# Turning the softmax's shares with VectorE and DMAs instead of TensorE in a one-core transformer block

## The chip, the cores and the metric

The kernel runs on one core of a Trainium2 chip. The metric is the device time of one execution in microseconds, the median of three runs. All data are float32. Engine names in the profile's lines: PE is TensorE (PEld its weight loads), DVE is VectorE, ACT is ScalarE, POOL is GpSimd, SP is SyncE, which here only issues DMAs (SPq in the timeline).

## The reference

A block of four layers on x of 8 x 512 x 256. The change touches the first, an attention with 16 query heads of 64 and one shared key and value head, a learned bias by relative position, a causal limit, and one "null" key and value ahead of the sequence:

```python
# per sequence b: x normalized over its 256 columns, then
q = l2norm(xn @ Wq) * q_scale          # (16, 512, 64)
k = l2norm(xn @ Wkv[:, :64]) * k_scale # (512, 64), one head for all
v = xn @ Wkv[:, 64:]                   # (512, 64)
# a null key and value (from cond_64) stand ahead of the sequence
sim  = 8 * q @ concat(null_k, k).T + concat(null_bias, rel_pos_bias)
attn = softmax(where(mask & causal, sim, -big))   # (16, 512, 513)
out  = layernorm((attn @ concat(null_v, v)) @ Wout) * g_out
```


## The kernel before, in words

Attention comes first and takes the time up to about 950 us; the delta rule and the experts share the rest. Attention works on tiles of 128 queries: 8 sequences, 4 tiles each (t = 0 to 3). Because of the causal limit a tile has n = (t + 1) * 128 keys. A tile's 8 pairs of heads are cut into steps of max(1, 4 // (t + 1)) pairs: 2, 4, 8 and 8 steps for the four tiles, 22 a sequence, 176 in all. A step handles some 1024 columns a partition (768 for t = 2): 2 * pairs heads, n keys each.

`attention_plan` writes the order out by hand. `units` holds the steps under way. `step(k)` calls, in this order: `attention_weights_turned` for step k, the due work of k - 0.5, `attention_softmax` for step k + AHEAD - 1, `attention_values` for step k - 1, `attention_scores` for step k + AHEAD, and the due work of k. Due work (queries, keys, normalizing, division, projection) is put at fractions of steps with `at(...)`. VectorE, ScalarE, SP and TensorE keep this order (class `Ordered`, and `a.mm` and `a.turn`, whose instructions all carry lines L125, L131 and L132); GpSimd's order is the scheduler's.

The steps' parts and their tiles:

- `attention_scores`: GpSimd adds bias and mask row into a_bm (L450, 3 buffers). TensorE multiplies turned queries a_qT by turned keys a_kT into two PSUM tiles a_s. VectorE adds a_bm and takes the minimum over each row in one instruction per head (the sign is turned round), into a_pr and a_mn.
- `attention_softmax`: ScalarE takes the exponential in place in a_pr, one instruction per head, with the row sums in a_rs.
- `attention_weights_turned`: TensorE turns every 128 x 128 block of a_pr (keys on partitions afterwards) into the PSUM tile a_ptp, two banks; ScalarE copies one half to a_pT, VectorE the other.
- `attention_values`: TensorE multiplies the values in a_kv by a_pT into a_av (PSUM), keys as the contracted dimension.
- `attention_shares`, `attention_shares_spread`, `attention_divided`: for each half of a tile's heads the inverse row sums are turned on TensorE into a_rp, copied to a_rT, written to DRAM (a_rd) by SP, and read back broadcast over 64 partitions, twice (a_rep, two issues on SP). VectorE multiplies a_av by a_rep into a_oT. `w.half` and `w.last` are the steps that end the halves.

A DMA that SP issues waits for the DMA eight issues before it on SP's queue (eight semaphores in turn). SP's queue also carries the loads of x and of the mask for the next sequence, and the stores of the layer's result hT.

Of the kernel before, what the change touches and what calls it, by code (L numbers as in the profile page):

```python
# [10 lines left out]
F32 = mybir.dt.float32  # L11
U8 = mybir.dt.uint8
AF = mybir.ActivationFunctionType
ALU = mybir.AluOpType
AX = mybir.AxisListType
PSUM = bass.MemoryType.PSUM
DRAM = bass.MemoryType.DRAM

P = 128
B, S, D = 8, 512, 256  # L20
NT = S // P
# [113 lines left out]

AHEAD = 3
KVW = 2 * DH + H1


def attention_setup(g, ctx, asides):
# [8 lines left out]
    a.wk = ctx.enter_context(tc.tile_pool(name="a_wk", bufs=2))  # L151
    a.sm = ctx.enter_context(tc.tile_pool(name="a_sm", bufs=3))
    a.s = ctx.enter_context(tc.tile_pool(name="a_s", bufs=4, space=PSUM))
    a.bias = wp.tile([P, H1, S], F32, name="a_bias")
    a.ks = wp.tile([P, 1], F32, name="a_ks")
    a.vw = wp.tile([H1, D], F32, name="a_vw")
    by_k = "(c p) n -> p c n"
# [1 line left out]
    with tc.tile_pool(name="as_c", bufs=1) as sp, tc.tile_pool(name="as_w", bufs=2) as wk, tc.tile_pool(  # L159
# [13 lines left out]
        w2 = sp.tile([P, NCT, H1], F32, name="as_w2")  # L173
        nc.scalar.dma_start(out=w2, in_=ins["c_w2"].rearrange(by_k, p=P))
        attention_plan(g, a, asides)
        a.run(-27)
        a.wkv = wp.tile([P, NCT, KVW], F32, name="a_wkv")
        a.sync.dma_start(out=a.wkv[:, :, 0 : 2 * DH], in_=ins["c_Wkv"].rearrange(by_k, p=P))
        a.wq = wp.tile([P, NCT, H1 * DH], F32, name="a_wq")
# [82 lines left out]
            )  # L262
            nc.vector.tensor_reduce(a.wkv[:, c, 2 * DH : KVW], wn, AX.X, ALU.add)

        a.run(-4)


        for h in range(H1):
            hk = wk.tile([P, S], F32, tag="hk", name="as_hk", bufs=4)
            row = gd[h]  # L270
            eng = a.sync if h % 2 else nc.scalar
            eng.dma_start(out=hk, in_=bass.AP(tensor=row.tensor, offset=row.offset, ap=[[1, P], [1, S]]))
            bp = ps.tile([P, 512], F32, tag="tp", name="as_bp")
            nc.tensor.matmul(bp, g.flip, hk, start=True, stop=True)
            nc.scalar.copy(a.bias[:, h, :], bp)


        nvb = sp.tile([P, 8 * H1], F32, name="as_nvb")
# [8 lines left out]
        nc.vector.tensor_copy(a.vw, vps[0:H1, 0:D])  # L287

    a.pp = ctx.enter_context(tc.tile_pool(name="a_pp", bufs=4))
    a.tr = ctx.enter_context(tc.tile_pool(name="a_tr", bufs=2, space=PSUM))  # L290
    a.av = ctx.enter_context(tc.tile_pool(name="a_av", bufs=2, space=PSUM))
    return a


def stats(g, a, x, mv, t):
# [39 lines left out]
def attention_norm(g, a, s):  # L335

    nc, b = a.nc, s.b
    r, mr = center(g, a, s.mv, "a_n")
    for t in range(NT):
        nc.scalar.activation(s.x[:, t, :], s.x[:, t, :], AF.Identity, bias=mr[:, t : t + 1], scale=r[:, t : t + 1])  # L340
    s.mrow = a.xp.tile([P, S], F32, tag="mrow", name=f"a_mrow{b}")
    nc.gpsimd.tensor_scalar(s.mrow, s.mk, 1.0, -BIG, ALU.subtract, ALU.mult)


def attention_turned(g, a, s):
# [33 lines left out]
def attention_keys_turned(g, a, s):  # L379
    nc = a.nc  # L380
    tp = a.s.tile([P, S], F32, tag="s", name="a_ktp")
    for t in range(NT):
        a.turn(tp[:, t * P : (t + 1) * P], s.kn[:, t].rearrange("p i d -> p (i d)"), g.ident)
    s.kT = a.xp.tile([P, S], F32, tag="kT", name=f"a_kT{s.b}")
    nc.scalar.activation(s.kT, tp, AF.Copy, scale=a.ks)
    s.hn = a.xp.tile([P, NT, D], F32, tag="hn", name=f"a_hn{s.b}")


# [36 lines left out]
def attention_queries_turned(g, a, w, half):  # L425

    nc = a.nc
    if half == 0:
        w.qT = a.wk.tile([P, 8, P], F32, tag="qT", name="a_qT")
        w.rs = a.sm.tile([P, H1], F32, tag="rs", name="a_rs")  # L430
        w.mn = a.sm.tile([P, H1], F32, tag="mn", name="a_mn")
        w.pn = a.sm.tile([P, H1], F32, tag="pn", name="a_pn")
        w.avs, w.rep = [None, None], [None, None]
    qf = w.q.rearrange("p h d -> p (h d)")
    tp = a.s.tile([P, 4, P], F32, tag="s", name="a_qtp")
    for i in range(4):
        cc = half * 4 + i
        a.turn(tp[:, i, :], qf[:, cc * P : (cc + 1) * P], g.ident)
    nc.scalar.copy(w.qT[:, half * 4 : half * 4 + 4, :], tp)


def attention_scores(g, a, w, c0, pairs):

    nc, s, t = a.nc, w.s, w.t
    n = (t + 1) * P
    u = SimpleNamespace(w=w, c0=c0, pairs=pairs, n=n)

    bm = a.pp.tile([P, 2 * S], F32, tag="bm", name="a_bm", bufs=3)
    bm = bm[:, 0 : 2 * pairs * n].rearrange("p (h m) -> p h m", m=n)
    nc.gpsimd.tensor_tensor(  # L450
        bm,
        a.bias[:, 2 * c0 : 2 * (c0 + pairs), (NT - 1 - t) * P :],
        s.mrow[:, 0:n].unsqueeze(1).to_broadcast([P, 2 * pairs, n]),
        ALU.add,
    )
    sps = [a.s.tile([P, S], F32, tag="s", name="a_s") for _ in range(2)]
    for j in range(pairs):
        for i in range(2):
            pi = slice(i * DH, (i + 1) * DH)
            a.mm(sps[i][:, j * n : (j + 1) * n], w.qT[pi, c0 + j, :], s.kT[pi, 0:n], start=True, stop=True)  # L460
    pr = a.pp.tile([P, 2 * S], F32, tag="pr", name="a_pr", bufs=5)
    u.pr = pr[:, 0 : 2 * pairs * n].rearrange("p (h m) -> p h m", m=n)
    for j in range(2 * pairs):
        h = 2 * c0 + j
        nc.vector.tensor_tensor_reduce(
            out=u.pr[:, j, :],
            in0=sps[j % 2][:, j // 2 * n : (j // 2 + 1) * n],
            in1=bm[:, j, :],
            scale=1.0,
            scalar=w.sn[:, h : h + 1],  # L470
            op0=ALU.add,
            op1=ALU.min,
            accum_out=w.mn[:, h : h + 1],
        )
    return u


def attention_softmax(g, a, u):
    nc, w = a.nc, u.w
    for j in range(2 * u.pairs):  # L480
        h = 2 * u.c0 + j
        nc.scalar.activation(
            u.pr[:, j, :], u.pr[:, j, :], AF.Exp, bias=w.mn[:, h : h + 1], scale=-1.0, accum_out=w.rs[:, h : h + 1]
        )


def attention_weights_turned(g, a, u):

    nc, n, kt, w = a.nc, u.n, u.n // P, u.w

    u.room = max(2, u.pairs)
    first = u.c0 % u.room
    if first == 0:
        w.pT = a.pp.tile([P, 4 * S], F32, tag="pT", name="a_pT", bufs=2)[:, 0 : 2 * u.room * n].rearrange(
            "p (i j m) -> p i j m", i=2, m=n
        )
    u.pT = w.pT
    m = u.pairs * n
    for i in range(2):
        tp = a.tr.tile([P, S], F32, tag="tr", name="a_ptp")  # L500
        for j in range(u.pairs):
            for k in range(kt):
                o = (j * kt + k) * P
                a.turn(tp[:, o : o + P], u.pr[:, 2 * j + i, k * P : (k + 1) * P], g.ident)
        copy = nc.vector.tensor_copy if i else nc.scalar.copy
        copy(u.pT[:, i, first : first + u.pairs], tp[:, 0:m].rearrange("p (j m) -> p j m", m=n))
    u.whole = first + u.pairs == u.room


def attention_values(g, a, u):  # L510

    w, kt = u.w, u.n // P
    c0 = u.c0 + u.pairs - u.room
    if c0 % 4 == 0:
        w.avs[c0 // 4] = a.av.tile([P, 4, P], F32, tag="av", name="a_av")
    for k in range(kt):
        for i in range(2):
            a.mm(
                w.avs[c0 // 4][i * DH : (i + 1) * DH, c0 % 4 : c0 % 4 + u.room, :],
                w.s.kv[:, k, DH : 2 * DH],  # L520
                u.pT[:, i, :, k * P : (k + 1) * P],
                start=k == 0,
                stop=k == kt - 1,
            )


def attention_shares(g, a, w, half):
# [10 lines left out]
def attention_shares_spread(g, a, w, half):  # L538
# [4 lines left out]
    rT = a.sm.tile([8, P], F32, tag="rT", name="a_rT")  # L543
    nc.scalar.copy(rT, tp[0:8, 0:P])
    rd = g.dram.tile([8, P], F32, tag="a_rd", name="a_rd", bufs=4)
    nc.sync.dma_start(out=rd, in_=rT)
    w.rep[half] = a.wk.tile([P, 4, P], F32, tag="rep", name="a_rep")
    for i in range(2):
        nc.sync.dma_start(out=w.rep[half][i * DH : (i + 1) * DH], in_=rd[i::2].partition_broadcast(DH))


def attention_divided(g, a, w, half):
# [42 lines left out]
def attention_plan(g, a, asides):  # L595
# [17 lines left out]
    def at(k, f, *args):  # L613
        due.setdefault(k, []).append((f, args))

    for w in tiles:
        b, t, s = w.s.b, w.t, w.s
        at(w.half - 2, attention_shares, w, 0)
        at(w.half - 0.5, attention_shares_spread, w, 0)
        at(w.half + 1, attention_divided, w, 0)  # L620
        at(w.last - 2, attention_shares, w, 1)
        at(w.last - 0.5, attention_shares_spread, w, 1)
        at(w.last + 1, attention_divided, w, 1)
        at(w.last + 1, attention_null_turned, w)
        at(w.last + 3, attention_projected, w)
        for half in range(2):
            at(w.first - 9 + half, attention_queries, w, half)
            at(w.first - 7.5 + half, attention_queries_normed, w, half)
            at(w.first - 5 + half, attention_queries_turned, w, half)
        if t == 0:  # L630
            at(w.first - 27, attention_load, s)
            for i in range(NT):
                at(w.first - 25 + i, attention_stats, s, i)
            at(w.first - 21, attention_norm, s)
            at(w.first - 16, attention_turned, s)
            at(w.first - 14, attention_keys, s)
            at(w.first - 10, attention_keys_turned, s)
        at(w.last + 5, attention_out_stats, s, t)
        if t == NT - 1:
            at(w.last + 5, attention_out_norm, s)  # L640
# [12 lines left out]
                a.outs.append(out)  # L653

    def step(k):
        if 0 <= k < len(steps):
            attention_weights_turned(g, a, units[k])
        given(k - 0.5)
        if 0 <= k + AHEAD - 1 < len(steps):
            attention_softmax(g, a, units[k + AHEAD - 1])  # L660
# [1437 lines left out]
```

## Time and profile before

| | us |
|---|---|
| Median of three runs (lowest to highest) | 2442.67 (2441.17 to 2445.53) |
| The profiled execution | 2440.13 |
| Its span | 2438.0 |
| Busy in the span: PE / DVE / ACT / POOL | 2294.3 / 1428.8 / 986.5 / 1126.6 |
| Span's mean granted TensorE clock | 0.969 |

The span is the time from the first to the last instruction of the profiled execution. Durations in lines of groups are ns for one instruction; "busy" is the union of a group's instructions. Matmuls are pipelined, so a group's busy time is less than its count times its mean. "Idle before" is the time its engine stood still just ahead of the group's instructions, with what ended that. A timeline line has its start, the duration, the engine, the line of the kernel and what is written from what. DMA issues are not counted as busy.

### The profile page before, as it was taken

The page shows a single profiled execution, that of the slowest core. Times are in us where ns is not written, and L with a number is a line of the kernel's source. Part 1 is how long each engine was busy: PE and PEld are TensorE (multiplying, and loading weights), DVE is VectorE, ACT ScalarE, POOL GpSimd, SP SyncE. Part 2 cuts the span into 40 slices and gives each one's busy share as a digit, 9 for nine tenths or more (in the row PEclk, how much of TensorE's full clock was granted, in tenths as well). Part 3 has the DMA queues.
Part 4 walks back from the last instruction along what each step waited for, and adds up shares of the span by engine and source line. Part 5 has one row for each costly group of instructions (what it writes and reads, how often), then busy time and mean ns, then how long its engine had stood idle before and what let it go on. Part 6 is the DMA issues. An engine that isn't in the chain of part 4 may idle for free.

```text
span 2438.0 us, 53093 instructions
## 1 busy us (share of the span) xinstructions
PE 2294.3 (94%) x20726; PEld 1686.7 (69%) x20726; DVE 1428.8 (59%) x4016; ACT 986.5 (40%) x2706; POOL 1126.6 (46%) x1420
## 2 busy tenths in 40 slices
PE   4899999999999997769899999999999999999999
PEld 2456665565666554547777788888887877888887
DVE  4456667665766675656646557467466466443433
ACT  2667666665766653333233323323223322311111
POOL 3677768677777762343324325225225234232211
PEclk8999999999999998769999999999999999999999
DMA  3201012010111014112323423334334134232433
GB/s 101 61 14 46 24 36 61 27 33 32 37 33 36 19 31 96 55 31 62 69 71 86 105 71 107 84 81 110 77 88 124 48 92 119 61 118 81 118 98 96
DMA packets 347082, 166.97 MB, mean 68 GB/s; under 512 B 195328, under 2 KB 325120, under 8 KB 346832
## 3 DMA queue, kind: packets, MB, share of 16 engines
q1 hardware_dynamic: 343824, 160.16, 24.4%
q10 hardware_dynamic: 3008, 3.43, 0.5%
q8 instruction: 163, 2.67, 0.5%
q14 instruction: 87, 0.71, 0.1%
HBM read 148.33 MB, written 15.18 MB: 67 GB/s over the span
## 4 chain that ended last, share of the span: by engine, by line
PE 72%; DVE 13%; DMA 5%; POOL 5%; ACT 2%; issue 2%; SPq 0%; ACTq 0%; DVEq 0%; POOLq 0%
PE m_guf L131 12%; PE m_gue L131 8%; PE m_accf L131 6%; PE a_op L131 6%; PE a_s L131 5%; PE a_av L131 5%; PE a_ptp L132 4%; PE a_qp L131 4%; PE m_acce L131 4%; PE d_pp L131 4%; DVE d_y L125 2%; PE d_op L131 2%; POOL a_bm L450 1%; DMA d_Uh<-d_hU 1%; PE d_cop L131 1%
## 5 line engine op out<-in xcount | busy, mean ns | idle before, releaser
L450 POOL TENSOR_TENSOR a_bm<-a_bias,a_mrow 128x1024 f32<-128x1024 f32 (+1 forms) x176 | 381.9, 2171 | 85.7 <-DVE a_mn L125 73.2
L131 PE MATMUL m_guf<-m_oute,m_wf 128*128 128x256 f32 x1536 | 370.9, 385 | 4.5 <-DVE m_hf L125 2.4
L131 PEld LDWEIGHTS m_guf<-m_oute,m_wf 128*128 128x128 f32 x1536 | 285.8, 191 | 58.5 <-issue 10.1
L131 PE MATMUL m_gue<-m_xT,m_we 128*128 128x256 f32 x1280 | 311.6, 387 | 3.2 <-DVE m_he L125 2.8
L125 DVE CUSTOM_DVE_ANT_0 a_pr<-a_s,a_bm,a_sn 128x512 f32<-128x512 f32 (+3 forms) x512 | 254.2, 545 | 68.9 <-PE a_s L131 53.5
L125 ACT ACTIVATE a_pr<-a_pr,a_mn 128x512 f32<-128x512 f32 (+3 forms) x512 | 282.0, 554 | 17.5 <-DVE a_mn L125 16.9
L125 POOL TENSOR_TENSOR m_hf<-m_hf,m_ctf 128x256 f32<-128x256 f32 x128 | 97.0, 759 | 374.5 <-DVE m_hf L125 186.2
L131 PEld LDWEIGHTS m_gue<-m_xT,m_we 128*128 128x128 f32 x1280 | 236.7, 191 | 39.5 <-DVE m_he L125 5.8
L125 DVE SCALAR_TENSOR_TENSOR m_tf<-m_tf,m_guf 128x256 f32<-128x256 f32 x192 | 80.4, 419 | 289.7 <-ACT m_tf L125 289.3
L125 POOL TENSOR_TENSOR m_he<-m_he,m_cte 128x256 f32<-128x256 f32 x128 | 104.6, 817 | 232.2 <-DVE m_he L125 106.7
L125 ACT ACTIVATE m_tf<-m_guf 128x256 f32<-128x256 f32 x192 | 73.4, 383 | 338.0 <-PE m_guf L131 333.4
L131 PE MATMUL a_s<-a_kT,a_qT 64*128 64x384 f32 (+3 forms) x1024 | 200.0, 471 | 6.3 <-DVE a_mn L125 6.0
L131 PE MATMUL m_accf<-m_hf,m_wf 128*128 128x256 f32 x768 | 197.4, 380 | 2.0 <-DVE m_outf L125 1.1
L132 PE MATMUL a_ptp<-table,a_pr 128*128 128x128 f32 x1280 | 179.7, 278 | 20.4 <-DVE a_pT L125 19.4
L132 PEld LDWEIGHTS a_ptp<-table,a_pr 128*128 128x128 f32 x1280 | 145.7, 142 | 75.2 <-issue 29.5
L125 DVE TENSOR_TENSOR m_te<-m_gue,m_te 128x256 f32<-128x256 f32 x160 | 67.6, 423 | 221.6 <-ACT m_te L125 221.6
L125 ACT ACTIVATE m_te<-m_gue 128x256 f32<-128x256 f32 x160 | 61.2, 382 | 294.7 <-PE m_gue L131 294.7
L131 PE MATMUL a_av<-a_pT,a_kv 128*64 128x256 f32 (+1 forms) x1216 | 167.0, 406 | 2.9 <-DVE a_pT L125 2.8
L131 PE MATMUL m_acce<-m_he,m_we 128*128 128x256 f32 x640 | 163.7, 381 | 0.6 <-issue 0.6
L131 PEld LDWEIGHTS m_accf<-m_hf,m_wf 128*128 128x128 f32 x768 | 145.7, 190 | 22.7 <-POOL m_hf L125 1.8
L131 PEld LDWEIGHTS a_s<-a_kT,a_qT 64*128 64x128 f32 x1024 | 84.0, 187 | 81.7 <-issue 40.2
L131 PEld LDWEIGHTS m_acce<-m_he,m_we 128*128 128x128 f32 x640 | 121.4, 191 | 18.0 <-issue 1.0
(343 smaller groups left out, 4076.8 us busy)
## 6 DMA issues: line engine op xcount, KB each, us to landing
a_rep<-a_rd SPq DMA_DIRECT2D x128, 128.0 KB
m_cte<-m_combe SPq DMA_DIRECT2D x64, 256.0 KB
m_ctf<-m_combf SPq DMA_DIRECT2D x128, 128.0 KB
m_we<-in_e_w_gate_dram SPq DMA_DIRECT2D x64, 128.0 KB
m_we<-in_e_w_up_dram SPq DMA_DIRECT2D x64, 128.0 KB
m_we<-in_e_w_down_dram SPq DMA_DIRECT2D x64, 128.0 KB
m_wf<-in_f_gate_w_dram SPq DMA_DIRECT2D x128, 64.0 KB
m_wf<-in_f_up_w_dram SPq DMA_DIRECT2D x128, 64.0 KB
```

Source lines behind the costliest of these rows:

```text
L125: return lambda *args, **kw: tc.keep_in_program_order(f(*args, **kw))
L131: mm = lambda *args, **kw: tc.keep_in_program_order(pe.matmul(*args, **kw))
L132: turn = lambda *args: tc.keep_in_program_order(pe.transpose(*args))
L450: nc.gpsimd.tensor_tensor(bm, a.bias[:, 2 * c0 : 2 * (c0 + pairs), (NT - 1 - t) * P :], s.mrow[:, 0:n].unsqueeze(1).to_broadcast([P, 2 * p ...
```

## The change

The blocks of a_pr are no longer turned on TensorE. VectorE turns each 32 x 32 block in place in a_pr (one instruction a step), and DMAs within SBUF bring the blocks to the other quarters of 32 partitions: quarter q and block b of a_pr go to partitions of quarter b in a_pT, 16 DMAs of 32 partitions for every two steps. So that whole blocks lie together, the keys are taken in another order: key k of every 128 lies in block k // 32, and bias, mask row, turned keys, a_bm and a_pr have a dimension of four blocks. a_pr covers two steps (3 buffers of 4 * S columns, before 5 of 2 * S), a_bm has 2 buffers, a_pT still 2. The turning runs for step k + AHEAD - 2 with AHEAD = 4, at the head of step k; the two PSUM banks of a_ptp go to a_av. The write of a_rd moves to ScalarE's queue, the two a_rep issues become a function of their own one step later (`attention_shares_brought`), and due work ahead of the steps moves up by one.

```diff
-AHEAD = 3
+AHEAD = 4
...
-            nc.scalar.copy(a.bias[:, h, :], bp)
+            nc.scalar.copy(quarters(a.bias[:, h]), by_block(bp))
...
-    a.tr = ctx.enter_context(tc.tile_pool(name="a_tr", bufs=2, space=PSUM))
-    a.av = ctx.enter_context(tc.tile_pool(name="a_av", bufs=2, space=PSUM))
+    a.av = ctx.enter_context(tc.tile_pool(name="a_av", bufs=4, space=PSUM))
...
+def by_block(x):
+    return x.rearrange("p (k b e) -> p b k e", b=4, e=CK)
+def quarters(x):
+    return x.rearrange("p b (k e) -> p b k e", e=CK)
...
 def attention_scores(g, a, w, c0, pairs):
...
-    u = SimpleNamespace(w=w, c0=c0, pairs=pairs, n=n)
-
-    bm = a.pp.tile([P, 2 * S], F32, tag="bm", name="a_bm", bufs=3)
+    u = SimpleNamespace(w=w, c0=c0, pairs=pairs, n=n, room=2 * pairs)
+    u.first = c0 % u.room
+    u.whole = u.first + pairs == u.room
+
+    bm = a.pp.tile([P, 2 * S], F32, tag="bm", name="a_bm", bufs=2)
...
-    pr = a.pp.tile([P, 2 * S], F32, tag="pr", name="a_pr", bufs=5)
-    u.pr = pr[:, 0 : 2 * pairs * n].rearrange("p (h m) -> p h m", m=n)
+    if u.first == 0:
+        pr = a.pp.tile([P, 4 * S], F32, tag="pr", name="a_pr", bufs=3)
+        w.pr = pr[:, 0 : 2 * u.room * n].rearrange("p (b h e) -> p b h e", b=4, h=2 * u.room)
+    u.pr = w.pr
...
 def attention_weights_turned(g, a, u):
-    for i in range(2):
-        tp = a.tr.tile([P, S], F32, tag="tr", name="a_ptp")
-        for j in range(u.pairs):
-            for k in range(kt):
-                o = (j * kt + k) * P
-                a.turn(tp[:, o : o + P], u.pr[:, 2 * j + i, k * P : (k + 1) * P], g.ident)
-        copy = nc.vector.tensor_copy if i else nc.scalar.copy
-        copy(u.pT[:, i, first : first + u.pairs], tp[:, 0:m].rearrange("p (j m) -> p j m", m=n))
...
+    nc, w = a.nc, u.w
+    x = u.pr[:, :, 2 * u.first : 2 * (u.first + u.pairs), :].rearrange("p b h e -> p b (h e)")
+    nc.vector.transpose(x, x)
+    if u.whole:
+        u.pT = a.pp.tile([P, 4 * S], F32, tag="pT", name="a_pT", bufs=2)[:, 0 : 2 * u.room * u.n].rearrange(
+            "p (q h e) -> p q h e", q=4, h=2 * u.room
         )
+        for q in range(4):
+            for b in range(4):
+                nc.sync.dma_start(
+                    out=u.pT[b * CK : (b + 1) * CK, q].rearrange("p h e -> p (h e)"),
+                    in_=u.pr[q * CK : (q + 1) * CK, b].rearrange("p h e -> p (h e)"),
+                )
...
-    nc.sync.dma_start(out=rd, in_=rT)
+    nc.scalar.dma_start(out=rd, in_=rT)
+    w.rd[half] = rd
+
+
+def attention_shares_brought(g, a, w, half):
     w.rep[half] = a.wk.tile([P, 4, P], F32, tag="rep", name="a_rep")
     for i in range(2):
-        nc.sync.dma_start(out=w.rep[half][i * DH : (i + 1) * DH], in_=rd[i::2].partition_broadcast(DH))
+        a.nc.sync.dma_start(out=w.rep[half][i * DH : (i + 1) * DH], in_=w.rd[half][i::2].partition_broadcast(DH))
...
-        at(w.half - 2, attention_shares, w, 0)
-        at(w.half - 0.5, attention_shares_spread, w, 0)
-        at(w.half + 1, attention_divided, w, 0)
+        at(w.half - 3, attention_shares, w, 0)
+        at(w.half - 1.5, attention_shares_spread, w, 0)
+        at(w.half - 0.5, attention_shares_brought, w, 0)
+        at(w.half + (1 if t else 2), attention_divided, w, 0)
...
     def step(k):
-        if 0 <= k < len(steps):
-            attention_weights_turned(g, a, units[k])
+        if 0 <= k + AHEAD - 2 < len(steps):
+            attention_weights_turned(g, a, units[k + AHEAD - 2])
```

The second half's due times (`w.last`) move in the same way, except that its division stays at `w.last + 1`. `attention_values` works on the larger a_pT: up to four pairs of heads a matmul, read in runs of 32.

## The prediction

> **What bounds the kernel now.** I read the page first (busy shares, slices), then the windows of the attention stage, then its groups, and last the DMA issues of SP's queue, since the change moves work there. The stage runs from about 85 to 950 us:
>
> ```profile
> core 0: us, PE busy (x) PEld busy (x) DVE busy (x) ACT busy (x) POOL busy (x), PEclk, DMA share, GB/s
> 85.00:950.00 865.00, 830.15 (x5065) 510.83 (x5065) 577.16 (x1696) 551.36 (x1661) 617.66 (x660) 0.99 0.12 34
> ```
>
> PE is busy for 830 of 865 us at a granted clock of 0.99; POOL (618), VectorE (577) and ScalarE (551) have room. There are 22 steps a sequence, 8 sequences, so 176 steps. I count in pairs of steps, because the changed kernel moves its data once for two: 88 pairs, 865/88 = 9.83 us each. The groups that go are these (after the count: busy us, mean ns, idle before):
>
> ```profile
> L132 PE MATMUL a_ptp<-table,a_pr 128*128 128x128 f32 x1280 | 179.7, 278 | 20.4 <-DVE a_pT L125 19.4
> ```
>
> and the copies of its result on VectorE, by form (ScalarE has as many):
>
> ```profile
> L125 DVE COPY a_pT<-a_ptp 128x512 f32<-128x512 f32 x112 | 75.2, 671 | 25.2 <-PE a_ptp L132 25.1
> L125 DVE COPY a_pT<-a_ptp 128x384 f32<-128x384 f32 x64 | 34.5, 539 | 1.2 <-PE a_ptp L132 1.2
> ```
>
> So the premise holds: the turning costs the bounding engine 180 us. The question is what takes its place. SP's queue in the timeline, beside VectorE's division that needs its result:
>
> ```profile
> 114.97 0.27 SPq L125 DMA_DIRECT2D a_rd<-a_rT  x1
> 116.23 1.24 SPq L125 DMA_DIRECT2D a_rep<-a_rd  x2
> ...
> 119.91 0.69 DVE L125 TENSOR_TENSOR a_oT<-a_av,a_rep 128x512 f32<-128x512 f32 x1 [0.38 <-DMA a_rep<-a_rd]
> ```
>
> The second column is how long SP is held by the issue itself: 0.62 us for one a_rep. VectorE waited for the landing, 119.91 - 117.47 = 2.44 us after the second issue ended. SP does only three such issues in 13 us today. How long SP is held by other shapes (min/median/max ns, from the tiles' views):
>
> ```profile
> L1534 SPq DMA_DIRECT2D m_ctf<-m_combf x128: 444/546/1685, 1248.4 to 2411.9; - x128
> L1534 SPq DMA_DIRECT2D m_cte<-m_combe x64: 319/376/1203, 1118.4 to 2338.6; - x64
> L1651 SPq DMA_DIRECT2D m_combf<-m_cT x8: 330/373/1401, 1245.8 to 2385.4; - x8
> L1651 SPq DMA_DIRECT2D m_combe<-m_cT x8: 292/298/299, 1116.9 to 2306.2; - x8
> ```
>
> All four move rows of 2 KB; they differ in rows: 64, 128, 16 and 8. It is not the bytes that hold SP.
>
> **What goes.** On PE 179.7 us of turning and most of the 20 us before it: 830 - 180 = 650, or 7.4 us a pair. On ScalarE 176 copies (94.7 us), on VectorE 176 (109.7 us). PSUM's two banks for the turning go to a_av.
>
> **What VectorE gets.** One transpose a step, 112 of 128x1024 and 64 of 128x768, in place in SBUF. The trace has no such operation. Nearest rows: the 128x1024 multiply of d_kn at 1.22 us; above it a_q's 128x512 multiply, mean 1.10 us, so 2.2 us for 1024, both from SBUF and lengthened in some places (0.81 to 1.63 us in the timeline); the dearest is one 128x1024 multiply at 3.36 us. Nothing goes below 1.1 us (two PSUM copies of 512 are 1.34). I take 1.22 and 0.95: one input, dense rows. Sum 112 x 1.22 + 64 x 0.95 = 198 us. VectorE then has 577 - 110 + 198 = 665 us, 7.6 us a pair, just over PE's 7.4; POOL stands at 618/88 = 7.0. With the idle that PE has today (4%) a pair bounded by the engines takes 7.9 us, and the stage 695: 170 us gained, if nothing else binds. A rule speaks against the change here: the Trainium skill ("VectorE: DVE Perf Modes", section The three transpose paths) gives 311 ns for a 128x128 turn in blocks of 32, which as my estimate would be 2.5 us for 1024 columns, nearer to the a_q row than to mine. The sum does not use it.
>
> **What SP gets.** After both steps of a pair are turned, 16 DMAs from quarter to quarter, 32 rows of 2 KB (1.5 KB for the third tile): 88 x 16 = 1408 issues, one queue, in order. a_rd (64 issues) moves to ScalarE's queue, about 64 x 0.33 = 21 us on an engine that loses 95, so nothing. The cost of an issue of 32 rows lies between the rows of 16 and of 64 (373 and 546 ns), plus 0.05 us between two issues in a chain: 0.42 to 0.60 us. I take the middle, 0.51; below it stands the 8-row DMA (0.30 + 0.05), above it the chained 64-row ones with a wait, 0.59 + 0.05 = 0.64; each new one carries a wait too, on a DMA eight before it. So 16 issues hold SP 16 x 0.51 = 8.2 us, against 7.9 us for a pair by the engines. The data are the smaller part: 1 MB a pair is 128 GB/s, and the 101 GB/s of the first slice took a DMA share of 0.35.
>
> Another rule speaks for it: the Trainium skill ("DMA: Bandwidth & Descriptors", section Issuing engines are not separate DMA queues) calls the sequencer's time to start a DMA usually small beside the DMA, and the same page's section Anatomy of one DMA has about 50 ns of dispatch, on another issue path. By that figure 16 issues would be 0.8 us (estimate), the engines would bound, and the kernel would take 2270 us. The rows above say 0.3 to 0.6 us, and decide.
>
> **What waits behind SP.** In the built order of the changed kernel SP has, in 56 of the 88 pairs (seven a sequence: two halves in each of four tiles, two of which fall together), 16 a_pT issues, then the two a_rep, then the next pair's a_pT. VectorE's order has the transpose that completes pair m, and before the one that completes pair m+1 stands the division a_oT, which waits for just that a_rep. That closes a loop across two engines: transpose -> 16 issues -> 2 a_rep issues (1.25) -> landing (2.44) -> a_oT (0.69) -> transpose (1.22). So such a pair can't take less than 16p + 5.6 us, where p is the time of one issue; at p = 0.51 it is 13.8 us, and today's whole pair is 9.83. The other 32 pairs take the larger of 7.9 and 16p = 8.2. Loads of x and mask and the stores of hT stand in the same queue, 24 issues in all, inside the error of p. Sum: 56 x 13.8 + 32 x 8.2 = 1035 us in place of 865, +170.
>
> **Edits at nothing.** a_bm is read in four blocks (rows of 128 and of 512 in one block took the same 2.37 us, so I expect no change) and has two buffers instead of three: POOL is then held by VectorE a step earlier; it has 2 to 3 us of room in a pair by the sum above, and if that cover is gone it costs some of the 73 us that it waits for a_mn already, as much again at most. a_av reads runs of 32; fewer and wider matmuls for the second tile, the same columns. VectorE's min-add writes four blocks instead of a row: same elements. The first one of a pair now waits for the DMAs of three pairs before; those are done unless SP is two pairs late. One step more of fill, about 5 us either way. PE will be busy for some 650 of 1035 us; the trace shows what such gaps do: between 975 and 1036 us PE was busy for 44 of 61 us at a granted clock of 0.71. 650/0.71 = 915 us still fits under 1035, so I charge nothing.
>
> **Rivals.**
> 1. SP's loop, p between 0.42 and 0.64 (my forecast). At 0.42: 56 x 12.3 + 32 x 7.9 = 942, +77, so 2517. At 0.64: 56 x 15.8 + 32 x 10.2 = 1211, +346, so 2786. For it: order of the queues and the issue rows. Against: no 32-row issue is in the trace, and none from SBUF to SBUF within it.
> 2. Faster: SP is held so shortly that the loop fits. Break-even is 56(16p + 5.6) + 32 x 7.9 = 865, p = 0.33 us, about what the 8-row DMA shows (0.30 + 0.05). At 0.25 it is 791, -74, 2366; from p = 0.14 down the engines bound, 695, -170, 2270. For it: rows of 8 and 16 are cheap, and the 128-row m_cte (376) is cheaper than the 64-row one, so the cost isn't plain in rows.
> 3. VectorE's transpose at the a_q rate, 2.2 us: the loop becomes 14.8, VectorE 9.6 a pair; 56 x 14.8 + 32 x 9.6 = 1136, +271, 2711.
> 4. Nothing to measure: p falls on the break-even point.
>
> That the change doesn't do what it says is excluded by the built order: no a_ptp is left on PE.
>
> **Numbers.** Chances: first 0.62, third 0.14, second 0.21, fourth 0.03. The profiled execution took 2440.1 us (span 2438.0) and the median of the runs is 2442.7, 2.5 above, so 2440.1 + 170 + 2.5 = 2613. The forecast's own range is 2520 to 2790. The range for 8 in 10 reaches into the second case, down to 2390 (p about 0.28), and up to 2790, which takes in the third. Measurement can tell about 0.2% (5 us) from no change: faster 0.21, same 0.03, slower 0.76.
>
> **What would show it.** Right: SPq a_pT issues of 0.4 to 0.6 us in unbroken rows of 16; VectorE idle before a_oT for a_rep of several us, some 56 times; PE in the stage at 60 to 70%, with a lower clock; transposes near 1.2 us. Wrong: a_oT waits for nothing, or issues under 0.33 us; then the stage ends before 950 us. If PE stays over 90% busy, rival 2 was right.

## The result, and the profile after

The changed kernel takes 2878.97 us (median of four runs, 2876.13 to 2882.34), the kernel before beside it 2443.0 (2441.17 to 2445.53): a ratio of 1.1785, 95% interval 1.177 to 1.1799. It is slower, as predicted, but by 436 us in place of 170, and outside the range. The profiled execution took 2876.5 us, its span 2874.7.

The attention stage, 85 to 952 us before, now ends near 1395 us; what follows it is within 6 us as long as before. The row of the windows for it (the columns are those of the first fence of the prediction):

```profile
85.00:1395.00 1310.00, 853.17 (x3662) 439.05 (x3661) 655.74 (x1702) 480.64 (x1489) 622.58 (x660) 0.79 0.34 87
```

No engine is busy for more than about 65% of the stage. PE's granted clock fell to 0.79, and still PE idles for 457 us. The page's slices show the same as a picture, the first 19 or so being attention:

```profile
PE   5666667566666666666578899999999999999998
PEclk8788888777887788777677999999999999999999
```

What new instructions cost, from the page's groups (us busy, mean ns, idle before) and, for SP, from the tiles' views (min/median/max ns of an issue):

```profile
L462 POOL TENSOR_TENSOR a_bm<-a_bias,a_mrow 128x1024 f32<-128x1024 f32 (+1 forms) x176 | 383.4, 2179 | 167.3 <-DVE a_mn L125 154.9
...
L125 DVE TENSOR_TENSOR a_oT<-a_av,a_rep 128x512 f32<-128x512 f32 x64 | 44.2, 691 | 416.3 <-DMA a_rep<-a_rd 409.4
...
L125 DVE STREAM_TRANSPOSE a_pr<-a_pr 128x1024 f32<-128x1024 f32 (+1 forms) x176 | 198.3, 1127 | 2.8 <-ACT a_pr L125 2.8
```

```profile
L125 SPq DMA_DIRECT2D a_pT<-a_pr x1408: 507/589/1632, 101.7 to 1388.0; - x176
L125 SPq DMA_DIRECT2D a_rep<-a_rd x128: 614/620/661, 111.9 to 1389.3; - x128
```

The transposes are cheap. An a_pT issue is not: 0.589 us, and with the 0.044 between two issues 0.633; a set of 16, the issues of one pair of steps, takes 10.1 us at the median, 10.36 on average. It isn't the wait for the DMA eight issues before that lengthens them: the last of a set has landed 1.4 us (median) after its issue, and the issue eight places later comes 5 us later. The waits name the loop from both ends, VectorE held by a_rep in the group of a_oT above, SP by VectorE here (us, times, longest; the longest, in the later views of this wait too, is that for the first transpose, ahead of the first set):

```profile
SPq L125 <- DVE a_pr L125: 259.2, 55, 19.4
```

One turn of it in the timeline (VectorE's and SP's rows; the bracket is the idle time before):

```profile
763.16 1.19 DVE L125 STREAM_TRANSPOSE a_pr<-a_pr 128x1024 f32<-128x1024 f32 x1
764.49 10.06 SPq L125 DMA_DIRECT2D a_pT<-a_pr  x16
...
774.59 1.29 SPq L125 DMA_DIRECT2D a_rep<-a_rd  x2
...
778.56 0.69 DVE L125 TENSOR_TENSOR a_oT<-a_av,a_rep 128x512 f32<-128x512 f32 x1 [7.96 <-DMA a_rep<-a_rd]
779.28 1.19 DVE L125 STREAM_TRANSPOSE a_pr<-a_pr 128x1024 f32<-128x1024 f32 x1
780.63 10.90 SPq L125 DMA_DIRECT2D a_pT<-a_pr  x16
```

From set to set 16.14 us: 10.1 of issues, 1.3 for a_rep, 2.7 until it has landed, 0.7 division, 1.2 transpose. VectorE stood still for 7.96 us with the next transpose behind the division. SP's rows from 102 to 1390 us fill the stage: sets 911 us, a_rep 83, pauses ahead of sets 250 (55 of them, 4.55 us each), loads, stores and small gaps 44, together 1288. Ahead of these lie 17 us until the first set, behind them 5 us.

### The profile page after: what moved, and what is told of

Read it like the earlier page. It is cut to its first block, busy times and chain, and to the rows that moved or that the text cites. A ratio compares the mean times of both kernels' runs of the same rounds, so it can differ in the third digit from the quotient of the medians.

```text
span 2874.7 us, 52513 instructions
## 1 busy us (share of the span) xinstructions
PE 2311.1 (80%) x19318; PEld 1613.1 (56%) x19318; DVE 1506.0 (52%) x4016; ACT 914.4 (32%) x2530; POOL 1130.3 (39%) x1420
## 4 chain that ended last, share of the span: by engine, by line
PE 40%; SPq 12%; DVE 9%; DMA 5%; issue 2%; ACT 1%; POOL 1%; DVEq 0%; POOLq 0%; ACTq 0%
SPq L125 12%; PE m_guf L131 10%; PE m_gue L131 7%; PE m_accf L131 5%; PE m_acce L131 3%; PE d_pp L131 3%; DMA a_rep<-a_rd 2%; DVE d_y L125 2%; PE d_op L131 1%; DMA d_Uh<-d_hU 1%; PE d_cop L131 1%; PE d_uwp L131 1%; PE d_mp L131 1%; DVE d_subst L125 1%; PE d_pw L131 1%
## 5 line engine op out<-in xcount | busy, mean ns | idle before, releaser
L462 POOL TENSOR_TENSOR a_bm<-a_bias,a_mrow 128x1024 f32<-128x1024 f32 (+1 forms) x176 | 383.4, 2179 | 167.3 <-DVE a_mn L125 154.9
L131 PE MATMUL a_av<-a_pT,a_kv 128*64 128x256 f32 (+1 forms) x1088 | 258.5, 637 | 101.5 <-DMA a_pT<-a_pr 96.4
L132 PE MATMUL a_rp<-table,a_rs 128*8 128x128 f32 x64 | 22.7, 354 | 315.6 <-DVE a_rs L125 309.9
L125 DVE TENSOR_TENSOR a_oT<-a_av,a_rep 128x512 f32<-128x512 f32 x64 | 44.2, 691 | 416.3 <-DMA a_rep<-a_rd 409.4
L131 PE MATMUL a_s<-a_kT,a_qT 64*128 64x384 f32 (+3 forms) x1024 | 237.8, 535 | 6.4 <-DVE a_mn L125 4.7
L131 PEld LDWEIGHTS a_av<-a_pT,a_kv 128*64 128x64 f32 x1088 | 114.7, 200 | 195.4 <-issue 163.3
L125 DVE STREAM_TRANSPOSE a_pr<-a_pr 128x1024 f32<-128x1024 f32 (+1 forms) x176 | 198.3, 1127 | 2.8 <-ACT a_pr L125 2.8
L131 PEld LDWEIGHTS a_s<-a_kT,a_qT 64*128 64x128 f32 x1024 | 99.9, 216 | 132.3 <-issue 53.2
```

Of the source, the lines that this page charges most:

```text
L125: return lambda *args, **kw: tc.keep_in_program_order(f(*args, **kw))
L131: mm = lambda *args, **kw: tc.keep_in_program_order(pe.matmul(*args, **kw))
L132: turn = lambda *args: tc.keep_in_program_order(pe.transpose(*args))
L462: nc.gpsimd.tensor_tensor(bm.rearrange("p h (b e) -> p h b e", b=4), a.bias[:, 2 * c0 : 2 * (c0 + pairs), :, S // 4 - e :], s.mrow[:, :, 0 ...
```

## The experiments

Theory 1: SP's issues, and the loop that they close through a_rep, set the time. Rivals: the landings or bytes; the engines themselves (clock, strided reads, transposes). The floor below is the time that the stage takes without the moves, 837 us; the way is the time from a pair's last transpose to its a_av. Runs without an interval are one profiled execution; the kernel before gave 2440.65 us on the chip of the first four.

### e_rep_act: a_rep on ScalarE's queue

```diff
-        a.nc.sync.dma_start(out=w.rep[half][i * DH ...
+        a.nc.scalar.dma_start(out=w.rep[half][i * DH ...
```

> The two a_rep issues go to ScalarE's queue; the 16 a_pT issues stay on SP. Theory 1 (SP's issues set the pace, 10.36 us for 16, and the loop through a_rep and the division adds the rest): the loop is cut, SP no longer waits for VectorE's transposes, and a pair takes 16p = 10.4 us; the stall of 273 us and the 83 us of a_rep issues go from SP, so 2879 - 273 - 83 = 2523 us (2500 to 2560). Rival 2 (engines set the pace: PE's lower clock and the strided reads, or VectorE's transposes): no change worth naming, 2830 to 2880. Rival 3 (the landing of the a_pT DMAs sets the pace of the 16): 2523 as well; it is told apart by the other runs.

Measured 2618.4 us. The loop is worth 258 us with the a_rep issues, not 356: SP still waits 53 us for transposes (the 72.8 of the view less the first wait), and the sets took 926 us in all.

```profile
SPq L125 <- DVE a_pr L125: 72.8, 28, 20.0
```

### e_rep_first: a_rep one place earlier on SP

```diff
-        at(w.half - 0.5, attention_shares_brought, w, 0)
+        at(w.half - 1, attention_shares_brought, w, 0)
...
-        at(w.last - 0.5, attention_shares_brought, w, 1)
+        at(w.last - 1, attention_shares_brought, w, 1)
```

> The two a_rep issues stay on SP but come one place earlier, ahead of the 16 a_pT issues that they followed. Theory 1: the loop through the division is cut, but SP still spends 1.29 us on them in 64 half tiles; 2879 - 273 = 2606 us (2580 to 2650), and VectorE no longer waits for a_rep. Rival (it is the load of SP's queue alone, and the order in it means nothing): no change, 2860 to 2890.

Measured 2662.5 us: 214 less than the changed kernel, by order alone. The same instructions stand in the same queue. VectorE's wait for a_rep ahead of a_oT falls from 409 us to 1.6. The rival "load, not order" falls; 56 us of the expected gain stay out, 20 of them again waits of SP for transposes.

### e_no_moves: no DMAs

```diff
-        u.pT = a.pp.tile(... name="a_pT", bufs=2) ...
-        for q in range(4):
-            for b in range(4):
-                nc.sync.dma_start(...)
+        u.pT = u.pr
```

> The 16 DMAs of a pair of steps are left out and a_av reads a_pr itself, so the blocks are not brought to the other quarters (the result is not the attention's); all engine work stays. It measures what the engines alone allow. By the prediction's sum 7.9 us a pair, a stage of 695 us, 2270 us (2250 to 2310) for the kernel. Rival (PE's lower granted clock is a cause, not a result of waiting; or a_av's strided reads cost as much as they seem to in the trace, 637 ns in place of 406): stage 800 us or more, 2380 us and up.

Measured 2413.6 us, 143 above the sum. The stage's row of the windows:

```profile
85.00:922.00 837.00, 736.07 (x3656) 388.62 (x3656) 657.68 (x1692) 474.18 (x1481) 621.88 (x659) 0.95 0.12 35
```

All the turning is off PE and the stage is 30 us shorter, not 170. PE is busy for 736 us where 830 - 180 is 650. The time lies in the rival's range, but not for the rival's reasons: the clock is 0.95, and a_av's reads in runs of 32 take 451 ns on average, where the means of before give 441 for this mix of widths. So even a free move would have been worth about 1%.

### e_rows128: the bytes in four issues

```diff
-            for b in range(4):
-                nc.sync.dma_start(out=u.pT[b * CK : (b + 1) * CK, q] ..., in_=u.pr[q * CK : (q + 1) * CK, b] ...)
+            nc.sync.dma_start(out=u.pT[:, q] ..., in_=u.pr[:, q] ...)
```

> The same bytes in 4 DMAs of 128 rows a pair of steps in place of 16 of 32 rows, each row staying on its partition (the quarters are not exchanged, so the result is not the attention's). Theory 1 (the number of issues): 4 issues of 0.35 to 0.65 us are 2 us a pair, the loop is 2 + 5.6 = 7.6, under the engines, so close to the run without moves, at most 30 us above it, 2270 to 2340. Rival 2 (bytes, or the landing of 1 MB a pair): the DMAs need as long as before, 2800 to 2880 us.

Measured 2409.5 us, level with no moves at all: bytes (135 GB/s over the stage) and landings cost nothing here. And the issue itself gives the failed price away: 128 rows hold SP as long as 32 do, 0.60 us.

```profile
L125 SPq DMA_DIRECT2D a_pT<-a_pr x352: 464/602/1807, 98.3 to 915.2; - x176
```

### e_shapes: 16, 32, 64 and 128 rows

```diff
-            for b in range(4):
-                nc.sync.dma_start(out=u.pT[b * CK : (b + 1) * CK, q] ..., in_=u.pr[q * CK : (q + 1) * CK, b] ...)
+            rows = 16 << q
+            for r in range(0, P, rows):
+                nc.sync.dma_start(out=u.pT[r : r + rows, q] ..., in_=u.pr[r : r + rows, q] ...)
```

> The same bytes as in the changed kernel, row by row on the row's own partition (the quarters are not exchanged, so the result is not the attention's), cut in four ways within each pair of steps: 8 DMAs of 16 rows, then 4 of 32, 2 of 64, 1 of 128. It measures the step of the prediction that priced an issue by its rows. If an issue has one price whatever its rows (the run with 4 DMAs of 128 rows points to it: 2.46 us for four), each place is held 0.59 to 0.65 us, the 15 issues are 9.5 us, and the time is one issue a pair less than after, 2879 - 88 x 0.63 = 2823 us. If the price goes by rows as the prediction had it: 8 x 0.42 + 4 x 0.51 + 2 x 0.60 + 0.43 = 7.0 us, and 2879 - 88 x 3.1 = 2606 us.

Measured 2819.8 us, 3 from the first figure. All issues together:

```profile
L125 SPq DMA_DIRECT2D a_pT<-a_pr x1320: 507/588/1813, 100.8 to 1329.9; - x189
```

Medians by place: 0.587 us for 16 rows, 0.588 for 32, 0.591 and 0.595 for 64, 0.596 for 128; the first of a set 0.572. Rows do not set the price.

### e_ends: where the two ends lie

```diff
+                if q == 1:
+                    out = pd[b * CK : (b + 1) * CK, 0:m]    # DRAM
+                if q == 2:
+                    in_ = xr[b * CK : (b + 1) * CK, 0:m]    # x, in DRAM
...
+        g.nc.gpsimd.memset(u.pT[:, 1], 0.0)
```

> 16 issues of 32 rows of 2 KB as in the changed kernel, on SP, each row on its own partitions, but four of them (places 4 to 7) write to DRAM and four (places 8 to 11) read x from DRAM (the result is not the attention's). It measures what an issue costs by where its two ends lie; the rows of before from which the prediction priced it all had one end in DRAM. If the price lies in the ends, places 0 to 3 and 12 to 15 are held 0.59 us and the others 0.30 to 0.43 (the run through DRAM had 0.34 for a write and 0.30 to 0.43 for reads), 16 issues are 8.2 us and the time is 2879 - 88 x 1.9 = 2710 us. If every issue in a chain costs the same, all are 0.59 and the time stays at 2860 to 2890.

Measured 2769.6 us. Three kinds of 32-row issue side by side on the same queue:

```profile
L125 SPq DMA_DIRECT2D a_pT<-a_pr x704: 507/588/1587, 101.0 to 1284.4; - x176
L125 SPq DMA_DIRECT2D a_pT<-in_x_dram x352: 311/420/1357, 105.6 to 1282.2; - x176
L125 SPq DMA_DIRECT2D a_pd<-a_pr x352: 308/427/1997, 103.5 to 1280.3; - x176
```

With both ends in SBUF an issue takes 0.588 us, with one in DRAM 0.42. So the ends matter, by 0.167 us, less than was expected: 8 x 0.167 x 88 = 118 us, and the time fell by 107 (2876.5 to 2769.6), the sets by 105 (911 to 806). The issue ahead matters too: the first write to DRAM, behind a move within SBUF, is held 0.578 us, and the first move behind a read from DRAM 0.512 (medians). The 0.373 us row of 16 in the kernel before was low because it ends in DRAM, not because it has 16 rows. Not all is said with that: a_rep, read from DRAM with a broadcast, takes 0.62.

### e_nm_bm3 and e_nm_turnless: what makes the floor of 837 us

On e_no_moves, a third a_bm buffer in the one, no transposes in the other:

```diff
-    bm = a.pp.tile([P, 2 * S], F32, tag="bm", name="a_bm", bufs=2)
+    bm = a.pp.tile([P, 2 * S], F32, tag="bm", name="a_bm", bufs=3)
```
```diff
-    nc.vector.transpose(x, x)
```

> The run without moves (16 DMAs left out, a_av reads a_pr; not the attention's result), and a_bm again with three buffers as before the change. GpSimd waited 81 us there for a_mn. If the missing buffer is what keeps the engines at 837 us for the stage in place of the 695 of the prediction's sum, the time falls by 40 us or more, to 2370 or less. Rival (other waits among the engines: a_rp on a_rs, a_s on ScalarE's copies): less than 15 us, 2400 to 2416.

> The run without moves, and VectorE's transposes left out too (a_av reads shares that are not turned; not the attention's result). It tells whether VectorE's new work is on the path. If PE sets the engines' floor (736 of 837 us busy), the time stays within 30 us of the 2413.6 of the run without moves. If VectorE's 198 us in its fixed order set it, up to 140 us go, to 2270, the prediction's floor.

Measured 2425.4 and 2393.7 us. Single runs of the kernel before on that chip lie between 2431 and 2444 us, so 12 more says no more than that the buffer is no cause; and of VectorE's 198 us only some 20 are on the path, within the 30 that were expected if PE sets the floor (single runs on two chips, so give or take some 10).

### e_nm_s6: more PSUM for the short tiles

```diff
-    a.av = ctx.enter_context(tc.tile_pool(name="a_av", bufs=4, space=PSUM))
+    a.av = ctx.enter_context(tc.tile_pool(name="a_av", bufs=2, space=PSUM))
+    a.s2 = ctx.enter_context(tc.tile_pool(name="a_s2", bufs=2, space=PSUM))
...
-    tp = a.s.tile([P, S], F32, tag="s", name="a_rp")
+    tp = a.s2.tile([P, S], F32, tag="s", name="a_rp")
...
```

> The run without moves (not the attention's result), with the two PSUM banks that the turning left given to a_rp, a_pntp and a_op in place of a_av, so that these no longer take turns with a_s, a_qp and a_qtp in four banks. If PE's floor in that run (837 us for the stage where the sum said 695) comes from waiting for PSUM banks, the time falls by 30 us or more, to 2380 or less. Rival (the fixed order over four engines that are all 60 to 90% busy; no single buffer): within 15 us of 2413.6.

Measured 2400.6 us: 13 less, within the spread of single runs, so not the cause either. What makes up the floor between the engines stays open.

### b_turnless: the kernel before without its turning

```diff
-    for i in range(2):
-        tp = a.tr.tile([P, S], F32, tag="tr", name="a_ptp")
-        ...
-                a.turn(tp[:, o : o + P], u.pr[:, 2 * j + i, k * P : (k + 1) * P], g.ident)
-        copy(u.pT[:, i, first : first + u.pairs], ...)
+    u.pT = u.w.pr.rearrange("p (c i) m -> p i c m", i=2)
```

> The kernel before, its turning on TensorE and the 352 copies left out (a_av reads a_pr unturned, so the result is not the attention's; a_pr covers two steps so that a_av keeps its shapes). It measures what the turning is worth to that kernel. By the prediction's sum, 180 us less on PE and 4% idle: 2440 - 170 = 2270 us. Rival (with PE below 90% the four engines in their fixed order wait for one another, as in the run without moves): 2380 to 2420 us, and the blocked layout is cleared. If it comes out between, the difference to 2413 is the layout's and VectorE's part.

Measured 2380.5 us, 59 below the kernel before beside it (2439.8). The old layout, no transposes, no copies, 180 us of matmuls gone:

```profile
85.00:890.00 805.00, 737.05 (x3806) 392.89 (x3804) 490.30 (x1527) 469.94 (x1489) 623.56 (x660) 0.96 0.13 36
```

PE's busy time is 737 us, 93 less and not 180, and PE's idle time grows from 35 to 68 us: hence 60 us and not 170. The trace of the kernel before shows where the other 87 us lie. Only for 137 of the 180 us of turning is no other matmul recorded; the other 43 lie under matmuls of other groups. And without the turning the other groups take 44 us more, a_av (167 to 198) and a_s (197 to 211) above all. Here a_pr is held until a_av has read it, which the kernel before does not need; what of the 59 that costs was not told apart. 33 us lie between this and e_no_moves; some 20 of them are the transposes by e_nm_turnless.

### e_split: five of the 16 issues on ScalarE

On e_rep_first:

```diff
-                nc.sync.dma_start(
+                (nc.scalar if 4 * q + b > 10 else nc.sync).dma_start(
```

> A correct version: a_rep ahead of the moves as in that run, and the last 5 of the 16 issues on ScalarE's queue, 11 on SP's. Theory 1: SP is held for 11 x 0.65 + 0.9 = 8.0 us a pair, ScalarE for 3.2 us more (480 + 280 of some 860 us), both under the engines' 9.5, so 2415 to 2460 us. Rival (ScalarE, waiting for VectorE's transpose ahead of its issues, holds up the exponentials behind them): 2480 us or more.

Measured 2663.6 us, no gain over e_rep_first, and the rival is right: ScalarE stands idle before its exponentials.

```profile
ACT a_pr L125 <- DMA a_pT<-a_pr: 429.6, 79, 8.6
```

The view names the a_pT DMA that landed last before, but the timeline shows what holds ScalarE: its own five issues, and the wait ahead of them.

```profile
643.30 0.20 ACT L125 ACTIVATE a_pn<-a_pn 128x8 f32<-128x8 f32 x1
646.20 3.10 ACTq L125 DMA_DIRECT2D a_pT<-a_pr  x5
649.33 0.26 ACT L125 COPY a_rT<-a_rp 8x128 f32<-8x128 f32 x1 [5.84 <-DMA a_pT<-a_pr]
```

Of the 5.84 us, 3.1 are issues; in the rest ScalarE's queue waits for VectorE's transpose, which ends at 646.05. Over the run the issues take 301 us and the idle time ahead of them 191.

### e_four: one set for four steps

On e_rep_first:

```diff
-    u = SimpleNamespace(w=w, c0=c0, pairs=pairs, n=n, room=2 * pairs)
+    u = SimpleNamespace(w=w, c0=c0, pairs=pairs, n=n, room=min(8, 4 * pairs))
...
-        pr = a.pp.tile([P, 4 * S], F32, tag="pr", name="a_pr", bufs=3)
+        pr = a.pp.tile([P, 8 * S], F32, tag="pr", name="a_pr", bufs=2)
...
-        u.pT = a.pp.tile([P, 4 * S], F32, tag="pT", name="a_pT", bufs=2)...
+        u.pT = a.pp.tile([P, 8 * S], F32, tag="pT", name="a_pT", bufs=1)...
...
-        at(w.half + (1 if t else 2), attention_divided, w, 0)
+        at(w.half + (2, 3, 1, 1)[t], attention_divided, w, 0)
```

> A correct version: a_pr and a_pT cover four steps in place of two (8 pairs of heads at most), so the 16 DMAs of 32 rows carry rows of up to 4 KB and come half as often, 96 issues a sequence in place of 176; a_rep ahead of them; a_pr 2 buffers, a_pT 1, a_oT and a_q2 1 for room. Theory 1 (issues cost, bytes do not): SP is held for 5.5 us a pair, below the engines' 9.5, so 2400 to 2440 us. Rival (work in lumps of four steps: a_av waits for 16 DMAs at once, a_pT's single buffer holds up the next set): 2470 us or more.

Measured 2663.2 us (2660.5 to 2670.5, four runs), 1.093 times before (1.0904 to 1.0956): nothing won over e_rep_first, though SP's sets fell from 915 to 501 us. Theory 1 in its plain form falls here, and the time is in the rival's range. SP now waits for VectorE, and PE for the set:

```profile
SPq L125 <- DVE a_pr L125: 366.0, 46, 19.4
```

```profile
PE a_av L131 <- DMA a_pT<-a_pr: 180.8, 37, 13.6
```

From a set's first issue to a_av pass 12.1 us (10.1 of issues, 2 of landing), and a_av waits for all 16. So issues can cost twice: as SP's time, and as time on the way, which the fixed order has to cover. That this is what holds e_four is argued, not shown: its work in lumps of four steps and its fewer buffers were not told apart from it.

### e_act_late: one step more before a_av

On e_rep_act:

```diff
-    w.rep[half] = a.wk.tile([P, 4, P], F32, tag="rep", name="a_rep")
+    w.rep[half] = a.wk.tile([P, 4, P], F32, tag="rep", name="a_rep", bufs=3)
...
-        at(w.half + (1 if t else 2), attention_divided, w, 0)
+        at(w.half + (2 if t else 3), attention_divided, w, 0)
...
-        at(w.last + 1, attention_divided, w, 1)
+        at(w.last + 2, attention_divided, w, 1)
...
-        if 0 < k <= len(steps):
-            u = units.pop(k - 1)
+        if 1 < k <= len(steps) + 1:
+            u = units.pop(k - 2)
```

> A correct version: the run with a_rep on ScalarE's queue (2618 us), and a_av, with the division behind it, one step later, so that 16 issues and a landing (12 us) have four steps in place of three before PE needs a_pT. If the rate of issue is what is left above the floor: 88 x 10.4 + 40 = 955 us for the stage, 2515 to 2560. If time on the way was no matter, 2605 to 2630.

Measured 2606.9 us, 12 less, where the second case had put it: time on the way was no matter here. The waits on transposes are gone but for the first, and SP is full; its sets now take 966 us, since SP also waits 63 us for landings of a_rep. Those are on ScalarE's queue, but the trace shows the two queues taking the same eight semaphores in turn, so an issue of SP can wait for a DMA of ScalarE:

```profile
SPq L125 <- DMA a_rep<-a_rd: 63.0, 45, 3.5
SPq L125 <- DVE a_pr L125: 19.6, 1, 19.6
```

With the loop taken out and a step more for the way, SP's queue still holds the stage at 1045 us, 208 above the floor; PE waits 177 us of it for a_pT.

### e_dram and e_dram_late: five issues through DRAM

On e_rep_act, and the same with the edit of e_act_late:

```diff
+        pd = g.dram.tile([P, 4, 2 * u.room * u.n // 4], F32, tag=f"a_pd{w.t}", name="a_pd", bufs=3)
+        nc.sync.dma_start(out=pd, in_=u.pr.rearrange("p b h e -> p b (h e)"))
+        for b in range(4):
+            nc.sync.dma_start(
+                out=u.pT[b * CK : (b + 1) * CK].rearrange("p q h e -> p q (h e)"),
+                in_=pd[:, b].rearrange("(q p) x -> p q x", q=4),
+            )
```

> A correct version with 5 issues in place of 16: a pair's a_pr is written to DRAM in one DMA of 128 rows and read back in 4 DMAs, one for each quarter of partitions, each with four rows of 2 KB a partition; a_rep on ScalarE's queue. Theory 1 (only SP's issues and the loop cost, the bytes do not): SP is held for 5 x 0.63 = 3.2 us a pair and a landing of 4 to 5 us, under the engines' 9.5 us, so near the run with 4 DMAs, 2400 to 2440 us, 0 to 2% faster than the kernel before. Rival (the second trip of the data, 2 MB a pair, or the longer way to a_av: 10 us from transpose to a_av): PE waits for a_pT, 2480 us or more.

Measured 2552.9 us (2549.6 to 2558.4), 1.0488 times before (1.0464 to 1.0511). The issues are as cheap as hoped:

```profile
L125 SPq DMA_DIRECT2D a_pd<-a_pr x88: 320/338/410, 101.2 to 1044.7; - x88
L125 SPq DMA_DIRECT2D a_pT<-a_pd x352: 302/425/1436, 106.3 to 1049.9; - x176
```

But the way is again 12 us (medians): 0.34 for the write, 4.2 until the first read, 1.7 of reads, 5.6 until a_av starts where it waits.

> A correct version: the run through DRAM (5 issues a pair, 2553 us), and a_av with the division one step later. If that run lost its time to the way from transpose to a_av (write 0.3 + landing 4.2 + reads 2.0 + landing 2 us = 9 us, PE waiting 135 us for a_pT): 2400 to 2450 us, faster than the kernel before or level with it. If it lost it to the double traffic (DMA share 0.7): 2520 us or more.

Measured 2532.5 us (2531.0 to 2535.7), ratio 1.0391 (1.0353 to 1.0428): 20 less, not 100, so giving the way one step more is worth little here too. SP, in order, waits for every write to land, and the next write stands behind that. And it waits for a_rep, which is on ScalarE's queue, by the semaphores that the two share:

```profile
SPq L125 <- DMA a_pd<-a_pr: 429.1, 74, 9.8
SPq L125 <- DMA a_rep<-a_rd: 186.1, 51, 8.1
```

### e_deep and e_deep_s6: reads behind the next write

```diff
         nc.sync.dma_start(out=pd, in_=u.pr...)
+        attention_weights_back(g, a)
+        a.away = (u, pd)
```

`attention_weights_back` issues the four reads of the pair before.

> A correct version: through DRAM, a_av one step later, and on SP's queue the four reads of a pair stand behind the write of the next pair, so that the write has a pair's time to land. If SP's waiting in order was what held the run with 2533 us, SP is held for 0.34 + 2.0 us a pair and waits for nothing in it, and the time falls to the floor of the run without moves or close above, 2405 to 2450 us. If the double traffic holds it (DMA share 0.7, landings of 5 us and more), it stays at 2500 us or more.

> The version before, with two of a_av's four PSUM banks given to a_rp, a_pntp and a_op. That was worth 13 us without moves; here 2390 to 2440 us, if a_av, which now needs its banks a step longer, does not miss them; if it does, slower than the version before by 10 us or more.

Measured 2645.0 us (ratio 1.0845, 1.0811 to 1.0878) and 2650.1 (1.0876, 1.0838 to 1.0915): over 110 us slower than e_dram_late. The wait moved:

```profile
SPq L125 <- DVE a_pr L125: 632.6, 85, 19.7
```

```profile
PE a_av L131 <- DMA a_pT<-a_pd: 232.5, 54, 15.7
```

The reads of a pair now stand behind the write of the next one, which waits for VectorE, which stands behind PE: a new loop, as read from these waits, and landings 6.6 us (median) after the last read, 5.3 in e_dram. How much is the loop and how much the doubled traffic (203 GB/s in e_dram_late) was not told apart. The two banks of e_deep_s6 gained nothing. No version here that does the whole attention beats the kernel before.

## Why the prediction was wrong, by its steps

The difference of 436 us, split by the runs: -27 from the kernel before to no moves (2440.7 to 2413.6), +205 for 16 issues a pair (e_rep_act), +44 for a_rep in the same queue (e_rep_first), +214 for the loop (the changed kernel).

- **The mechanism** is right: SP's loop, in the forecast's order of stations. 56 turns of it were predicted and 55 found (no pair follows the last), with VectorE idle 55 times before a_oT, PE busy 65% of the stage and the clock lower. e_rep_first shows it, since order alone is worth 214 us.
- **The price of an issue is the step that failed.** It was read as a matter of rows, between 16 rows (0.373) and 64 (0.546), 0.51 with the gap. It is 0.633 (0.647 with the pauses inside a set): 16 and 128 rows cost the same (e_shapes), and one end in DRAM makes it cheaper (e_ends). The upper bound of 0.64 comes near, but from reads of DRAM with a broadcast, another kind of issue. In the sum: (10.36 - 8.16) x 88 = 194 of the 275 us by which the stage (1310) is longer than the forecast's 1035. With the measured price alone the forecast's own equation gives 1225 us for the stage and 2803 for the kernel, just above its range; the terms that follow make up the rest.
- **The rest** is in terms called small or left out. The "24 issues inside the error of p", with the loads for the later layers and the small gaps, took 44 us. Until the first set and after the last a_rep pass 22 us. a_rep is issued in 64 half tiles, not 56 (13 us). A pause of SP is 4.55 us and not 2.44 + 0.69 + 1.22 = 4.35, one pause fewer (7 us). These give 280 with the 194, against 275; the forecast's sum was rounded up by 3.
- **The engines' floor** of 7.9 us a pair was wrong too: it is 837/88 = 9.5. It doesn't bear on the measured time, since a set of issues takes 10.36; in the forecast's sum it would have put 9.5 for 8.2 in 32 pairs, 42 us more. The step is "on PE 179.7 us of turning": 830 - 180 = 650 with today's 4% idle. Without its turning the kernel before keeps 737 us busy and wins 59 us. A group's busy time was taken for what goes with the group: 43 of the 180 us lie under other groups' matmuls, and the other groups take 44 us more without it (b_turnless). So rival 2 could at best have brought 2410 and not 2270, and with 9.5 in its equation the break-even price falls from 0.33 to 0.28 us.
- **VectorE's transposes**: 198 us predicted, 198.3 measured, 1.22 us for 128x1024. The row taken was one of several between 1.1 and 3.4 us and no run had tested the choice, so that it hit to 0.01 us is partly luck. The Trainium skill ("VectorE: DVE Perf Modes", section The three transpose paths) with its 311 ns for 128x128, there in bf16, would have given 2.5 us (estimate); the trace, in float32, shows half of that, and rival 3 fell with it.
- **The rule that spoke for the change** (the Trainium skill, "DMA: Bandwidth & Descriptors", section Issuing engines are not separate DMA queues: a start's time on the sequencer is usually small beside the DMA) misleads here. One issue holds SP for 0.59 us and its DMA has landed 1.4 us later (median of the last of each set; 1.3 to 3.0), but the holds of 16 in one queue add up to 10.1 us and the landings overlap.
- **Edits at nothing**: a_bm in blocks is free (2179 ns, before 2171 by the group), its third buffer too (e_nm_bm3). Bytes are free (e_rows128). a_av became dearer, 637 ns on average for 406: with the same reads, 256 columns take 580 ns here at a granted clock of 0.62 while they run, and 413 in e_no_moves at 0.95. PE idles 457 us of the stage, so it was covered.

## What to carry to other kernels

Count the DMA issues of a queue and price each by a chained issue of the same kind (same ends, same broadcast) and not by a neighbour in rows or bytes; then ask also whether the way from producer to consumer is covered (here one step more was worth only 12 and 20 us). Before taking work off the busiest engine, ask what the next floor is: leaving the work out altogether, which takes one run, showed 59 us where the busy time said 180. In a queue that is in order, put what another engine waits for ahead of the long set, not behind it.

## What the runs showed of the hardware

A DMA issue on SP takes 0.59 us in a chain from SBUF to SBUF, whether 16, 32, 64 or 128 rows of 1.5 or 2 KB (e_shapes); 0.42 to 0.43 us with one end in DRAM (e_ends, e_dram), and 0.30 to 0.34 there after a pause (e_dram); 0.62 for a_rep, read from DRAM with a broadcast. A write of 1 MB to DRAM was waited for 4.2 us after its issue (e_dram), moves within SBUF had landed 1.3 to 3.0 us after the last issue of a set. Matmuls that overlap others in the record (43 of 180 us in a_ptp) do not give their busy time back when they go.
